# Edge weights of a two-layer graph attention kernel, computed per group of four edge tiles instead of per pair

## The chip, the cores and the metric

The kernel runs on one core of one Trainium2 chip. The metric is device microseconds of that core for one execution; the time given for a kernel is the median of its runs. A core has five engines that run their own instruction queues in order and wait for each other through semaphores: TensorE (PE: matmuls; PEld: its weight loads), VectorE (DVE), ScalarE (ACT), GpSimd (POOL) and SyncE (SP). Data comes from and goes to device memory through DMAs, which SP, ACT and POOL issue.

## The reference

The input is a table x of 6250 nodes with 768 numbers each, and 100000 edges (src, dst), sorted by dst. x is normalised and rectified, goes through two layers of graph attention and two dense layers, and is added to itself. Cut to what matters:

```python
def gat_conv(x, src, dst, W, a_src, a_dst, bias, heads):
    h = (x @ W).reshape(n, heads, -1)
    alpha_s = (h * a_src[None]).sum(-1)
    alpha_d = (h * a_dst[None]).sum(-1)
    e = leaky_relu(alpha_s[src] + alpha_d[dst], 0.2)
    m = segment_max(e, dst);  e = exp(e - m[dst])
    denom = segment_sum(e, dst)
    alpha = e / (denom[dst] + 1e-16)
    return segment_sum(h[src] * alpha[:, :, None], dst).reshape(n, -1) + bias

h = relu(layernorm(x))
h = relu(gat_conv(h, src+loops, dst+loops, W1, ..., heads=4))   # 768 -> 256
h = relu(gat_conv(h, src+loops, dst+loops, W2, ..., heads=1))   # 256 -> 256
out = x + relu(h @ Wm1 + bm1) @ Wm2 + bm2                       # 256 -> 768
```

## The kernel before, in words

**The weight of an edge.** The maximum over a segment cancels in the quotient, so the kernel doesn't subtract it. It also takes a factor out that depends on dst alone: with s the source score and d the destination score, exp(leaky_relu(s + d)) divided by exp(d) is max(exp(s), exp(0.2 s) · rho), with rho = exp(-0.8 d). The weight of an edge is therefore two exponentials of the source score (e1 and e2, on ScalarE), one product with rho and one maximum (both on VectorE). Each source row in the table of a layer carries its score behind its features, so that one gather brings both.

**Stages.** First come the features of all 49 node tiles of 128 nodes (line 414 and after). Then `layer_edges` (line 529) runs once per layer over the edges. Edges are cut into tiles of 128, four tiles make a group, and there are NG = 196 groups, of which the first has only its last two tiles. Groups 4t to 4t+3 share one PSUM tile `e_ps[t]`, in which `meet` puts, through small matmuls with a 0/1 mask, rho of every edge in three bf16 parts, and `join` adds the parts. The later thirds of this tile hold v and, in layer 1, the weight w.

**One group.** The order of work is written out by hand, in the loop from line 706; no scheduler moves it. In iteration g every engine gets its instructions in this order: `gather(g + 8)` issues four indirect DMAs on POOL (line 553), each of which brings 128 rows for one tile of the group eight ahead; `pair(g, 0)` works on the first two tiles of group g; `advance` runs a piece of the work on node tiles that are complete; `make_hot(g + 1)` (layer 1, line 583) builds the 0/1 matrices of the next group; depending on g mod 4 come `meet`, `ahead` (line 785) or, in layer 1, `make_mask` (line 572); then `pair(g, 1)` for the other two tiles, `advance` again, `join` every fourth time, and `gather_up(g - 2)` (lines 673 and 681), which adds the group's sums from PSUM to the running sum.

**A pair.** `pair` issues two exponentials (lines 620 and 622), the product v (line 625) and the maximum w (line 628 in layer 2, line 635 in layer 1). In layer 1 it then scales the two gathered tiles by w in one instruction (line 637), and TensorE multiplies by the 0/1 matrices `hot`. In layer 2 it builds a weighted 0/1 matrix per tile (line 632), and TensorE multiplies it by the gathered rows. Both end in two matmuls per pair into `o_ps` (line 648).

**Buffers.** Gathered rows have 20 buffers of two tiles, ten groups in all. The instructions of a gather wait for the last readers of their buffer, and for the landing of the gather eight before. The small tiles e1, e2 and w have four buffers each, `hw` has eight, `o_ps` three.

**Node work.** When the 128 nodes of a tile are complete, `node.steps` normalises them (lines 791 to 804 in layer 1; 896 to 911 in layer 2), transposes them and multiplies. Layer 1 writes the row table of layer 2 (line 817), from which the gathers of layer 2 read; layer 2 ends in the dense layers and the output (lines 937 to 946). The first few gathers of each layer read only rows that are written early (line 300), and a matmul adds what they miss (lines 273 and 275).

Of the kernel before, what the change touches and what calls it, by code (L numbers as in the profile page):

```python
# [10 lines left out]
F32 = mybir.dt.float32  # L11
BF16 = mybir.dt.bfloat16
I32 = mybir.dt.int32
AF = mybir.ActivationFunctionType
# [3 lines left out]
P = 128  # L18
# [3 lines left out]
HID = 256  # L22
OUT_DIM = 768
SLOPE = 0.2
# [5 lines left out]
TPG = 4  # L30
NG = NQ
# [22 lines left out]
def kernel(  # L54
# [21 lines left out]
    nc = tc.nc  # L76
# [56 lines left out]
    RW = {1: 4 * (HID // 4 + 1), 2: HID + 2}  # L133
# [99 lines left out]
    for layer in EARLY:  # L233
        n = len(THERE[layer])
# [294 lines left out]
    def layer_edges(layer, H, node, pre, matched, pre_pool):  # L529
# [4 lines left out]
        with tc.tile_pool(name=f"eg{layer}", bufs=4) as eg, \  # L534
                tc.tile_pool(name=f"hw{layer}", bufs=8) as hwp, \
                tc.tile_pool(name=f"sum{layer}", bufs=4) as sums, \
                tc.tile_pool(name=f"sm{layer}", bufs=4) as sm:
            G, hot, e_ps, o_ps = {}, {}, {}, {}

            def tiles(g):  # L540

                return range(max(TPG * g, FIRST) - TPG * g, min(TPG * g + TPG, LAST) - TPG * g)
# [61 lines left out]
            def join(t):  # L604
                if t >= NT:
# [4 lines left out]
                    e_ps[t][:, T, 3 * H:4 * H],  # L610
                    e_ps[t][:, T, :3 * H].rearrange("p t (h k) -> p t h k", k=3), AX.X, ALU.add)

            def pair(g, p):

                if 2 * p not in tiles(g):
                    return
                Gp = G.pop(TPG // 2 * g + p)
                sc = Gp[:, :, RW[1]:] if layer == 1 else Gp[:, :, HID:HID + 1]
                e1 = sm.tile([P, 2, H], F32, name="e1")
                nc.scalar.activation(e1, sc, AF.Exp)  # L620
                e2 = sm.tile([P, 2, H], F32, name="e2")
                nc.scalar.activation(e2, sc, AF.Exp, scale=SLOPE)  # L622
                at = TPG * (g % 4) + 2 * p
                rho, v, w = (e_ps[g // 4][:, at:at + 2, k * H:(k + 1) * H] for k in range(3, 6))
                nc.vector.tensor_mul(v, e2, rho)  # L625
                if layer == 2:
                    w = sm.tile([P, 2, H], F32, name="w")
                    nc.vector.tensor_max(w, v, e1)  # L628
                    hw = hwp.tile([P, 2, P], F32, name="hw")
                    for t in range(2):  # L630
                        k = TPG * g + 2 * p + t
                        nc.vector.tensor_scalar(hw[:, t], iota_ps, dcol[:, k:k + 1], w[:, t],  # L632
                                                ALU.is_equal, ALU.mult)
                else:
                    nc.vector.tensor_max(w, v, e1)  # L635
                    hw = hwp.tile([P, 2, H, C + 1], F32, name="hw")
                    nc.vector.tensor_mul(  # L637
                        hw, Gp[:, :, :RW[1]].rearrange("p t (h c) -> p t h c", h=H),
                        w.unsqueeze(3).to_broadcast([P, 2, H, C + 1]))
                if g not in o_ps:  # L640
                    o_ps[g] = ps.tile([P, RW[layer]], F32, name="o_ps", tag="o", bufs=3)
                for t in range(2):
                    k = 2 * p + t
                    if layer == 2:
                        l, r = hw[:, t], Gp[:, t]
                    else:
                        l, r = hot[g][:, k], hw[:, t].rearrange("p h c -> p (h c)")
                    nc.tensor.matmul(o_ps[g], l, r[:, :RW[layer]], start=(k == tiles(g)[0]),  # L648
                                     stop=(k == TPG - 1))
# [56 lines left out]
            for g in range(NG):  # L706
                t, j = divmod(g, 4)
                if g == NG - 2:
                    at_end.append(g)
                gather(g + AHEAD)  # L710
                pair(g, 0)
                if g == NG - 1:
                    pair(g, 1)
# [20 lines left out]
                if g < NG - 1:  # L734
                    pair(g, 1)
# [35 lines left out]
    with tc.tile_pool(name="w2p", bufs=1) as wp, tc.tile_pool(name="wk2", bufs=2) as wk:  # L771
# [48 lines left out]
        with tc.tile_pool(name="pre1", bufs=1) as pre:  # L820
            first_hits(pre, 1, 0)
            pre1 = prepare(pre, 1, 4)
            layer_edges(1, 4, Node1(), pre1,
                        lambda: scores_in(ps, w2, *w2_in, KH, 1), pre)


    with tc.tile_pool(name="wmp", bufs=1) as wp, tc.tile_pool(name="x3", bufs=4) as xp, \
# [122 lines left out]
        for stage in range(2):  # L950
            first_hits(pre, 2, stage)
        layer_edges(2, 1, Node2(), pre2, matched, pre)

    edges_stack.close()
# [298 lines left out]
```

## Time and profile before

| | us |
|---|---|
| median of 3 runs (2609.17 to 2623.1) | 2619.84 |
| profiled execution, its own time | 2137.04 |
| its span, from first to last instruction | 2135.3 |
| POOL busy in the span | 1600.6 |
| PE busy | 1589.5 |
| DVE busy | 1416.1 |
| ACT busy | 593.1 |
| mean granted TensorE clock | 0.825 |

The profile is of one execution. Its own time is 1.7 us above its span, and 482.8 us below the median of the runs: a ratio of 2619.84 to 2137.04, which is 1.226. The page has only one execution in detail, so durations are those of the faster one. "Busy" is the time in which an engine was executing, and not its issuing of instructions. A line of the groups' view names a line of the kernel, the engine and operation, what is written and read with its shape, how often; then the busy time in total and the mean of one in ns, and behind the last bar the idle time of the engine just before these instructions, with what ended it. A line of the timeline gives the start, the duration, the engine, the line and operation, and in brackets the idle time before it.

### The profile page before, as it was taken

The page shows a single profiled execution, that of the slowest core. Times are in us where ns is not written, and L with a number is a line of the kernel's source. Part 1 is how long each engine was busy: PE and PEld are TensorE (multiplying, and loading weights), DVE is VectorE, ACT ScalarE, POOL GpSimd, SP SyncE. Part 2 cuts the span into 40 slices and gives each one's busy share as a digit, 9 for nine tenths or more (in the row PEclk, how much of TensorE's full clock was granted, in tenths as well). Part 3 has the DMA queues.
Part 4 walks back from the last instruction along what each step waited for, and adds up shares of the span by engine and source line. Part 5 has one row for each costly group of instructions (what it writes and reads, how often), then busy time and mean ns, then how long its engine had stood idle before and what let it go on. Part 6 is the DMA issues. An engine that isn't in the chain of part 4 may idle for free.

```text
span 2135.3 us, 26701 instructions
## 1 busy us (share of the span) xinstructions
PE 1589.5 (74%) x6763; PEld 1075.4 (50%) x6765; DVE 1416.1 (66%) x4359; ACT 593.1 (28%) x2601; POOL 1600.6 (75%) x1759
## 2 busy tenths in 40 slices
PE   8996777766767677666768677777767777777777
PEld 6874444444444444444445445545545545545544
DVE  7887777667677777677777655555555555555554
ACT  4651222222222222222222222222222222222222
POOL 6877777777777777777777777777777777777774
PEclk9998888677777767887779888888888888888888
DMA  9976666555555565565556455565555555565553
GB/s 356 363 232 206 169 172 176 165 169 163 167 170 163 170 170 162 169 168 158 166 143 211 130 180 166 169 181 166 169 181 166 169 181 166 169 181 167 168 171 114
DMA packets 157544, 383.26 MB, mean 179 GB/s; under 512 B 35543, under 2 KB 49966, under 8 KB 157382
## 3 DMA queue, kind: packets, MB, share of 16 engines
q0 software_dynamic: 75072, 209.10, 36.6%
q1 hardware_dynamic: 80940, 170.88, 23.1%
q10 hardware_dynamic: 1370, 1.48, 0.2%
q8 instruction: 58, 0.95, 0.2%
q14 instruction: 104, 0.85, 0.1%
HBM read 323.13 MB, written 58.19 MB: 179 GB/s over the span
## 4 chain that ended last, share of the span: by engine, by line
DMA 27%; PE 26%; DVE 26%; issue 9%; ACT 7%; POOL 5%; ACTq 0%; SPq 0%; POOLq 0%; DVEq 0%
DMA G<-table,src_i 26%; PE o_ps L648 11%; DVE hw L637 8%; PE y_ps L937 7%; POOL G L553 4%; PE h_ps L350 4%; DVE acc L673 3%; DVE e_ps L625 3%; ACT sum L681 3%; DVE e_ps L635 2%; ACT e L620 2%; DVE hw L632 2%; DVE mask L572 1%; ACT e L622 1%; PE y_ps L873 1%
## 5 line engine op out<-in xcount | busy, mean ns | idle before, releaser
L553 POOL DMA_INDIRECT G<-table,src_i x1545 | 1470.1, 952 | 472.3 <-issue 260.5
L648 PE MATMUL o_ps<-hw,hot 128*128 128x260 f32 x1564 | 596.7, 520 | 282.9 <-DVE hw L637 221.4
L648 PE MATMUL o_ps<-G,hw 128*128 128x258 f32 x1564 | 469.1, 432 | 229.8 <-DVE hw L632 229.1
L648 PEld LDWEIGHTS o_ps<-hw,hot 128*128 128x128 f32 x1564 | 352.9, 248 | 492.9 <-DVE hw L637 359.2
L625 DVE TENSOR_TENSOR e_ps<-e,e_ps 128x8 f32<-128x8 f32 (+1 forms) x782 | 128.4, 164 | 598.9 <-ACT e L622 597.5
L648 PEld LDWEIGHTS o_ps<-G,hw 128*128 128x128 f32 x1564 | 309.9, 212 | 348.3 <-DVE hw L632 290.5
L681 ACT ACTIVATE sum<-acc 32x260 f32<-32x260 f32 (+1 forms) x384 | 159.9, 416 | 776.9 <-DVE acc L673 775.3
L620 ACT ACTIVATE e<-G 128x8 f32<-128x8 f32 (+1 forms) x782 | 159.9, 204 | 617.8 <-DMA G<-table,src_i 576.4
L632 DVE TENSOR_SCALAR hw<-iota_ps,dcol,w 128x128 f32<-128x128 f32 x782 | 285.0, 406 | 14.4
L637 DVE TENSOR_TENSOR hw<-G,e_ps 128x520 f32<-128x520 f32 x391 | 271.9, 695 | 15.2 <-DVE e_ps L635 2.0
L937 PE MATMUL y_ps<-wm,mT 128*128 128x384 f32 x392 | 206.5, 664 | 0.7 <-ACT mT L926 0.7
L673 DVE SCALAR_TENSOR_TENSOR acc<-acc,keep,o_ps 128x260 f32<-128x260 f32 (+1 forms) x388 | 184.5, 476 | 0.1
L622 ACT ACTIVATE e<-G 128x8 f32<-128x8 f32 (+1 forms) x782 | 148.9, 190 | 0.2
L350 PE MATMUL h_ps<-w,r 128*128 128x256 f32 x588 | 133.0, 380 | 4.4 <-ACT r L341 4.4
L583 DVE TENSOR_TENSOR hot<-iota_ps,dcol 128x512 f32<-128x512 f32 (+1 forms) x196 | 133.5, 682 | 0.0
L937 PEld LDWEIGHTS y_ps<-wm,mT 128*128 128x128 f32 x392 | 88.3, 249 | 66.9 <-issue 40.9
L350 PEld LDWEIGHTS h_ps<-w,r 128*128 128x128 f32 x588 | 108.0, 190 | 21.8 <-ACT r L341 5.7
L635 DVE TENSOR_TENSOR e_ps<-e_ps,e 128x8 f32<-128x8 f32 x391 | 68.1, 174 | 13.4
L365 POOL TENSOR_TENSOR ha<-kept,a1b 128x512 f32<-128x512 f32 x45 | 53.2, 1183 | 23.9 <-ACT kept L356 23.8
L628 DVE TENSOR_TENSOR w<-e_ps,e 128x2 f32<-128x2 f32 x391 | 62.2, 159 | 13.3
L601 PEld LDWEIGHTS <-mask 128*128 128x128 bf16 x1564 | 57.7, 101 | 11.4 <-issue 1.7
L767 ACT ACTIVATE rT<-tp,bT 128x128 f32<-128x128 f32 x196 | 59.4, 352 | 6.6 <-PE tp L761 6.4
(405 smaller groups left out, 1137.7 us busy)
## 6 DMA issues: line engine op xcount, KB each, us to landing
xt<-in_x SPq DMA_DIRECT2D x96, 384.0 KB, 4.8
drow<-dmod_d SPq DMA_DIRECT2D x49, 512.0 KB, 6.4
mask_d<-mask SPq DMA_DIRECT2D x98, 256.0 KB, 2.2
mask<-mask_d SPq DMA_DIRECT2D x98, 256.0 KB, 5.9
G<-table,src_i POOLq DMA_INDIRECT x1545, 2.9
xTt<-in_xT SPq DMA_DIRECT2D x49, 384.0 KB, 5.9
out<-y SPq DMA_DIRECT2D x48, 384.0 KB
table<-kept SPq DMA_DIRECT2D x49, 132.0 KB, 3.7
```

The source lines that it names most:

```text
L350: nc.tensor.matmul(h_ps, r[:, k], w1[:, k], start=(k == 0), stop=(k == KI - 1))
L553: nc.gpsimd.indirect_dma_start(out=G[k // 2][:, k % 2], out_offset=None, in_=table[layer], in_offset=bass.IndirectOffsetOnAxis(ap=src_i[:, ...
L583: nc.vector.tensor_tensor(hot[g][:, T[0]:T[0] + n], iota_ps.unsqueeze(1).to_broadcast([P, n, P]), dcol[:, k:k + n].unsqueeze(2).to_broadca ...
L620: nc.scalar.activation(e1, sc, AF.Exp)
L622: nc.scalar.activation(e2, sc, AF.Exp, scale=SLOPE)
L625: nc.vector.tensor_mul(v, e2, rho)
L632: nc.vector.tensor_scalar(hw[:, t], iota_ps, dcol[:, k:k + 1], w[:, t], ALU.is_equal, ALU.mult)
L637: nc.vector.tensor_mul(hw, Gp[:, :, :RW[1]].rearrange("p t (h c) -> p t h c", h=H), w.unsqueeze(3).to_broadcast([P, 2, H, C + 1]))
L648: nc.tensor.matmul(o_ps[g], l, r[:, :RW[layer]], start=(k == tiles(g)[0]), stop=(k == TPG - 1))
L673: nc.vector.scalar_tensor_tensor(acc, run[0], keep[:, k:k + 1], o_ps.pop(g), ALU.mult, ALU.add)
L681: nc.scalar.activation(done[t][r], acc[r], AF.Copy)
L937: nc.tensor.matmul(y_ps, mT[:, j], wm2[:, j, s * half:(s + 1) * half], start=False, stop=(j == KH - 1))
```

## The change

A new function `weigh(g, pairs)` works out the weights of all tiles of a group at once. It is called from `pair(g, 0)` with both pairs (in group 0 from `pair(0, 1)`, with the only pair that is there), and its results wait in a dictionary for the two pairs. The last two groups (g >= NG - 2) call it once per pair, as before. The exponentials stay one per pair and kind, but all four of a group now stand together, ahead of the first product; the product and the maximum are one instruction each over four tiles. What follows in `pair` is unchanged, and so is the order of the loop around it. The tiles e1, e2 and w are twice as wide, in as many buffers.

```diff
+            def weigh(g, pairs):
+
+                pairs = [p for p in pairs if 2 * p in tiles(g)]
+                n = 2 * len(pairs)
+                e1 = sm.tile([P, TPG, H], F32, name="e1")
+                e2 = sm.tile([P, TPG, H], F32, name="e2")
+                for k, p in enumerate(pairs):
+                    Gp = G[TPG // 2 * g + p]
+                    sc = Gp[:, :, RW[1]:] if layer == 1 else Gp[:, :, HID:HID + 1]
+                    nc.scalar.activation(e1[:, 2 * k:2 * k + 2], sc, AF.Exp)
+                    nc.scalar.activation(e2[:, 2 * k:2 * k + 2], sc, AF.Exp, scale=SLOPE)
+                at = TPG * (g % 4) + 2 * pairs[0]
+                rho, v, w = (e_ps[g // 4][:, at:at + n, k * H:(k + 1) * H] for k in range(3, 6))
+                nc.vector.tensor_mul(v, e2[:, :n], rho)
+                if layer == 2:
+                    w = sm.tile([P, TPG, H], F32, name="w")[:, :n]
+                nc.vector.tensor_max(w, v, e1[:, :n])
+                for k, p in enumerate(pairs):
+                    weights[g, p] = w[:, 2 * k:2 * k + 2]
+
             def pair(g, p):
 
                 if 2 * p not in tiles(g):
                     return
-                Gp = G.pop(TPG // 2 * g + p)
-                sc = Gp[:, :, RW[1]:] if layer == 1 else Gp[:, :, HID:HID + 1]
-                e1 = sm.tile([P, 2, H], F32, name="e1")
-                nc.scalar.activation(e1, sc, AF.Exp)
-                e2 = sm.tile([P, 2, H], F32, name="e2")
-                nc.scalar.activation(e2, sc, AF.Exp, scale=SLOPE)
-                at = TPG * (g % 4) + 2 * p
-                rho, v, w = (e_ps[g // 4][:, at:at + 2, k * H:(k + 1) * H] for k in range(3, 6))
-                nc.vector.tensor_mul(v, e2, rho)
+                if g >= NG - 2:
+                    weigh(g, (p,))
+                elif (g, p) not in weights:
+                    weigh(g, (0, 1))
+                Gp, w = G.pop(TPG // 2 * g + p), weights.pop((g, p))
                 if layer == 2:
-                    w = sm.tile([P, 2, H], F32, name="w")
-                    nc.vector.tensor_max(w, v, e1)
                     hw = hwp.tile([P, 2, P], F32, name="hw")
...
                 else:
-                    nc.vector.tensor_max(w, v, e1)
                     hw = hwp.tile([P, 2, H, C + 1], F32, name="hw")
```

More of the change, by code (lines that the diff above doesn't have):

```diff
@@ L537, in layer_edges @@
                 tc.tile_pool(name=f"sm{layer}", bufs=4) as sm:
-            G, hot, e_ps, o_ps = {}, {}, {}, {}
+            G, hot, e_ps, o_ps, weights = {}, {}, {}, {}, {}
             def tiles(g):
```

## The prediction

> **What bounds the kernel now.** I read the busy shares first, then the waits of POOL, then stretches out of both layers, the groups, and last the timeline. The page has POOL and PE level:
>
> ```profile
> PE 1589.5 (74%) x6763; PEld 1075.4 (50%) x6765; DVE 1416.1 (66%) x4359; ACT 593.1 (28%) x2601; POOL 1600.6 (75%) x1759
> ```
>
> A quarter of POOL seems to be idle. Its waits say what that is (total us, times, longest):
>
> ```profile
> POOL G L553 <- issue: 260.5, 855, 0.4
> POOL G L553 <- ACT e L622: 41.4, 136, 0.3
> POOL G L553 <- PE o_ps L648: 37.5, 123, 0.3
> ```
>
> 855 waits of 0.3 us each, none longer than 0.4, and the others have the same 0.3 us under whatever name happened to be last. That is a fixed cost between two gathers. The timeline of POOL, in both layers, confirms it:
>
> ```profile
> 714.55 0.95 POOL L553 DMA_INDIRECT G<-table,src_i  x1 [0.30 <-issue]
> 715.80 0.95 POOL L553 DMA_INDIRECT G<-table,src_i  x1 [0.30 <-issue]
> ...
> 2109.43 0.95 POOL L553 DMA_INDIRECT G<-table,src_i  x1 [0.30 <-ACT mT L926]
> 2110.68 0.95 POOL L553 DMA_INDIRECT G<-table,src_i  x1 [0.30 <-issue]
> ```
>
> A gather starts every 1.25 us, from 144.6 us to 2110.7 us: 1564 gathers (1545 of line 553, 19 of line 300) x 1.25 = 1955 us, and the stretch is 1966. One real wait is in it, 1.89 us at 1146.8 us between the layers. So the span is 144.6 before the first gather, 1966 of gathers without another pause, and 24.6 after the start of the last. The chain that ended last names POOL's line with 4% only, and the gathers' DMA with 26%, because it follows data; but the data comes when POOL has issued it.
>
> The others have room in each layer (busy us in 200 us of layer 1, then of layer 2, in the order PE, PEld, DVE, ACT, POOL):
>
> ```profile
> 640.00:840.00 200.00, 142.47 (x540) 94.09 (x539) 143.63 (x401) 49.39 (x240) 151.56 (x160) 0.73 0.59 167
> 1440.00:1640.00 200.00, 150.01 (x680) 100.41 (x680) 113.60 (x410) 54.78 (x250) 151.28 (x161) 0.84 0.58 172
> ```
>
> A group takes four gathers, 5.00 us. Of these DVE works 143.63/200 x 5.00 = 3.59 us in layer 1 and 2.84 in layer 2, PE 3.56 and 3.75. They follow the gathers at the heel; nothing holds POOL back.
>
> [...]
>
> ```profile
> 730.57 0.48 DVE L572 TENSOR_SCALAR mask<-drow,pidx 128x1024 bf16<-128x1024 bf16 x1
> 730.80 1.06 POOL L553 DMA_INDIRECT G<-table,src_i  x1 [0.30 <-DVE hot L583]
> ...
> 734.57 0.42 DVE L791 TENSOR_TENSOR all__7316<-mine,sum 128x260 f32<-128x260 f32 x1
> ...
> 734.67 1.14 POOL L553 DMA_INDIRECT G<-table,src_i  x1 [0.30 <-ACT e L622]
> ```
>
> A gather that starts under the mask, or under a sum of two SBUF tiles, comes 1.37 and 1.44 us before its successor. I went through all spacings: 55 are between 1.30 and 2.3 us, and lose 10.3 us together, 0.19 each; nearly all stand beside lines 572, 791, 804, 785 or 896.
>
> **The change, part by part.**
>
> *Removed on DVE.* The groups give
>
> ```profile
> L635 DVE TENSOR_TENSOR e_ps<-e_ps,e 128x8 f32<-128x8 f32 x391 | 68.1, 174 | 13.4
> L625 DVE TENSOR_TENSOR e_ps<-e,e_ps 128x8 f32<-128x8 f32 x391 | 65.0, 166 | 225.7 <-ACT e L622 225.1
> L625 DVE TENSOR_TENSOR e_ps<-e,e_ps 128x2 f32<-128x2 f32 x391 | 63.4, 162 | 373.2 <-ACT e L622 372.4 <-DVE rden L908 0.5
> L628 DVE TENSOR_TENSOR w<-e_ps,e 128x2 f32<-128x2 f32 x391 | 62.2, 159 | 13.3
> ```
>
> Six elements more cost the product 4 ns, 0.67 each; so I estimate 171 and 180 ns at 16 elements, 163 and 160 at 4. A group of layer 1 had 2 x (166 + 174) = 680 ns and will have 351, one of layer 2 642 and 323. With 193 groups that change (not the first and the last two): 193 x (329 + 319) ns = 125 us and 772 instructions fewer. On the path: 0, since POOL's next gather doesn't wait for them. If that cover were gone, they would be worth up to 125 us.
>
> *The exponentials* stay four per group at 190 to 207 ns: 0.
>
> *The added wait.* The product for pair 0 now needs all four gathers, two cadences or 2.5 us more. Behind it in DVE's queue stand the scaling of pair 0, `hot`, the mask, node work and `gather_up`; in ACT's queue, behind the exponentials of pair 1, stand the sums (line 681), rT, o and mT, and PE waits for these. All of it comes up to 2.5 us later, and does again in every group, without adding up: after the landing DVE has 3.59 - 0.33 = 3.26 us of work in 5.00, PE 3.56 or 3.75. Only POOL could turn lateness into time. Its waits are for the readers of a buffer ten groups old (8 groups ahead of use, 40 us) and for the landing of the gather eight before (10 us; landing takes 2.9). 2.5 us don't reach either. Cost 0; without these buffers it would be up to 2.5 x 194 x 2 = 970 us. No DMA is moved on SP's or POOL's queue; stores and masks of SP come up to 2.5 us later, and the masks of layer 2 are read a layer later.
>
> *The seam and the end.* The last two groups of a layer go per pair as before. At the seam the exponentials of layer 1's last pair wait 2.62 us for their data, so a delay of group 193 is used up before it. At the end I count -0.4 to +1 us: the consumer is behind there, and DVE has 0.33 us less to do. Together -1 to +2.5, I take 0.
>
> *Lockout.* [...] 97 masks and four lines of about 49, 293 in all, of which 55 now hit, 19%. Their places against the cadence change. Bounds: none hits, -10 us; all hit, 293 x 0.19 - 10 = +45. In between I argue from the phase. The exponentials that waited for a landing mostly start 0.3 to 0.5 us after a gather's start. All work of a group now starts from there, and a group is exactly four cadences, so that phase is more fixed than before. In an odd group: product at 0.4 + 0.34, scaling of pair 0 at 1.15, `hot` 0.62 later, and the mask at 1.77 + 0.61 = 2.38, which is 1.13 into a cadence, and the next gather starts under it at 1.25. About a quarter of masks hit now; I take half: 97 x 0.25 x 0.19 = +4.6 us. The others I leave, so +4.
>
> Sum, against the profiled execution: 2137 + 0 + 0 + 4 = 2141 us.
>
> **From there to the median.** The median of the runs is 1.226 times the profiled time. [...] I read the runs as the same kernel, bound by the same gathers, at that ratio; no trace here shows it. 2141 x 1.226 = 2624.
>
> **The rivals.** 0.5% is about what a measurement of this kernel can tell from no change: 13 us of the runs, or 10.7 of the profile.
>
> 1. *As forecast*, within 0.5%: 2607 to 2633.
> 2. *Slower through lockout.* The fixed phase puts masks and sums under gathers in most groups. For: above. Against: landings scatter by some us[...]. From 55 hits to 112 it decides: 57 x 0.19 = 10.7 us; all 293 hits would give 2137 + 45 = 2182, or 2675. I put it at about 2645.
> 3. *Faster.* The runs, which no profile shows, are bound by DVE and not by POOL. Then up to 125 x 1.226 = 153 us go: 2467. Against: DVE is at 3.59 of 5.00 us, and would have to be slower by 1.39 times where POOL isn't.
> 4. *Slower through the clock.* PE's work now comes in one burst per group. [...] If it fell below 0.84 x 3.75/5.00 = 0.63 in layer 2, PE would need more than a group's 5.00 us. At 0.5 it needs 6.30: 196 x 1.30 = 255 us, 2137 + 255 = 2392, or 2930. Against: the gap per group is only 5.00 - 3.75 = 1.25 us.
>
> **Chances.** Case 1 has 0.74, case 2 0.17, case 3 0.06 (with lockout gone and more), case 4 0.03. So faster 0.06, same 0.74, slower 0.20. The range of 8 in 10 takes in most of case 2: 2607 to 2650.
>
> **What would show it.** POOL's spacing of 1.25 us and its first and last gather within some us of before, and DVE busy near 1290 us with 3587 instructions, while the span stays: right. What DVE saves should come back as idle time before the product v. More than 112 spacings above 1.30 us, or POOL busy above 1612: case 2. Waits of POOL over 0.4 us, for PE or DVE, in the middle of a layer: the cover that I count on isn't there. PEclk below 0.63: case 4. A median that moves without the profile's span would mean that the runs are bound by something else.

## The result, and the profile after

The changed kernel takes 2647.11 us (median of 4 runs, 2640.82 to 2652.78), beside 2618.53 us for the kernel before (4 runs): a ratio of 1.0117, with an interval of 1.0092 to 1.0142. It is slower by 1.2%. The time lies within the forecast range, but outside the likeliest case, which said no change. The profiled execution of the changed kernel took 2648.64 us, with a span of 2646.9; so this time the profile is one of a run like the timed ones.

The busy shares of the changed kernel:

```profile
PE 1623.4 (61%) x6763; PEld 1120.4 (42%) x6765; DVE 1290.9 (49%) x3587; ACT 561.5 (21%) x2601; POOL 1598.9 (60%) x1759
```

VectorE did 772 instructions and 1416.1 - 1290.9 = 125.2 us less, as forecast. POOL was busy just as long as before, 1598.9 us against 1600.6, yet the span is 511.6 us longer than that of the profile before. POOL stood still instead. The waits (total us, times, longest us) show it, and also where VectorE stood:

```profile
POOL G L553 <- issue: 763.9, 1303, 7.7
...
DVE acc L686 <- remote: 412.9, 48, 17.8
```

In the profile of before POOL's longest wait in this row was 0.4 us; here it is 7.7. The busy time in 200 us of layer 1, then of layer 2 (order PE, PEld, DVE, ACT, POOL):

```profile
640.00:840.00 200.00, 108.60 (x432) 73.30 (x432) 104.56 (x255) 34.64 (x187) 121.01 (x127) 0.72 0.47 132
1440.00:1640.00 200.00, 114.97 (x499) 80.15 (x499) 83.44 (x271) 34.73 (x171) 125.20 (x132) 0.75 0.47 136
```

127 and 132 gathers instead of 160 and 161. No engine is busy throughout. The timeline of POOL and then of VectorE, around one of the pauses of layer 1, shows who waits for whom:

```profile
760.93 0.94 POOL L553 DMA_INDIRECT G<-table,src_i  x1 [0.30 <-issue]
762.17 0.95 POOL L553 DMA_INDIRECT G<-table,src_i  x1 [0.30 <-issue]
769.45 1.07 POOL L553 DMA_INDIRECT G<-table,src_i  x1 [6.33 <-issue]
```

```profile
756.63 0.69 DVE L650 TENSOR_TENSOR hw<-G,e_ps 128x520 f32<-128x520 f32 x1
766.09 0.48 DVE L686 SCALAR_TENSOR_TENSOR acc<-acc,keep,o_ps 128x260 f32<-128x260 f32 x1 [8.77 <-remote]
767.58 0.18 DVE L626 TENSOR_TENSOR e_ps<-e,e_ps 128x16 f32<-128x16 f32 x1 [1.01 <-ACT e L623]
767.79 0.18 DVE L629 TENSOR_TENSOR e_ps<-e_ps,e 128x16 f32<-128x16 f32 x1
768.01 0.70 DVE L650 TENSOR_TENSOR hw<-G,e_ps 128x520 f32<-128x520 f32 x1
```

Where POOL does run, gathers are 0.95 us long and 1.25 us apart, as in the profile before. Then VectorE waits 8.77 us before the sum `acc`, whose input comes from TensorE. POOL goes on until all its buffers are full: counted from the trace, it is then 36 to 40 tiles ahead of the scaling, and 40 is what the buffers hold. At 763.1 us it stops. When `acc` has started at 766.09, the order is `acc`, the sum and four exponentials on ScalarE (from 766.61 to 767.55 us, for which VectorE waits 1.01 us), product, maximum, scaling; only the scaling frees a buffer, and the next gather starts 769.45 - 766.09 = 3.36 us after the start of `acc`. I call this stretch the restart. From this `acc` to the next late one, at 792.36 us, it is 26.3 us, for sixteen gathers that take 20.0. So in these stretches VectorE and what it waits for set the pace, and POOL follows.

"remote" stands where the trace finds no instruction whose end fits the signal that ended the wait. The signal itself is in the trace: it is TensorE's, at 766.06 us, 0.03 us before `acc` starts; five more follow up to 766.36, and none is recorded from 748.48 up to it. TensorE's work had been done long before:

```profile
749.23 1.14 PE L661 MATMUL o_ps<-hw,hot 128*128 128x260 f32 x4 [0.38 <-DVE hw L650]
...
757.68 1.04 PE L661 MATMUL o_ps<-hw,hot 128*128 128x260 f32 x4
768.76 3.56 PE L661 MATMUL o_ps<-hw,hot 128*128 128x260 f32 x8 [10.04 <-DVE hw L650]
```

The matmuls that this `acc` adds up (those of the group two before) end with the first line, at 750.37 us, 15.7 us before `acc` starts, and TensorE is idle from 758.72 us on. VectorE waits over 2 us before `acc` 45 times in layer 1 of this trace, and each time these matmuls had ended 10 to 25 us before. Six signals within 0.3 us can't be the ends of matmuls of which four take 1.1 us. So, by the records of its instructions, TensorE's signals come late here, and not its work.

The profile before shows nothing of this: there POOL led the scaling by some 4 to 8 tiles only, in both layers. It is the profile of a run of another kind than those whose median was given.

### The profile page after: what moved, and what is told of

The parts are those of the page before. It is cut to its first block, busy times and chain, and to the rows that moved or that the text cites. A ratio compares the mean times of both kernels' runs of the same rounds, so it can differ in the third digit from the quotient of the medians.

```text
span 2646.9 us, 25778 instructions
## 1 busy us (share of the span) xinstructions
PE 1623.4 (61%) x6763; PEld 1120.4 (42%) x6765; DVE 1290.9 (49%) x3587; ACT 561.5 (21%) x2601; POOL 1598.9 (60%) x1759
## 4 chain that ended last, share of the span: by engine, by line
issue 24%; DVE 23%; PE 23%; another core or an unknown queue 20%; ACT 7%; DMA 2%; POOL 1%; ACTq 0%; DVEq 0%; SPq 0%; POOLq 0%
PE o_ps L661 10%; DVE hw L650 5%; PE y_ps L950 5%; DVE hot L583 4%; PE h_ps L350 4%; DVE hw L646 3%; ACT sum L694 3%; DVE acc L686 2%; ACT e L622 2%; DVE e_ps L626 2%; DMA G<-table,src_i 2%; PE tp L934 1%; DVE mask L572 1%; ACT e L623 1%
## 5 line engine op out<-in xcount | busy, mean ns | idle before, releaser
L661 PE MATMUL o_ps<-hw,hot 128*128 128x260 f32 x1564 | 573.5, 507 | 562.2 <-DVE hw L650 370.6
L661 PE MATMUL o_ps<-G,hw 128*128 128x258 f32 x1564 | 487.8, 449 | 182.3 <-issue 115.3
L661 PEld LDWEIGHTS o_ps<-G,hw 128*128 128x128 f32 x1564 | 338.3, 226 | 295.7 <-issue 150.9
L686 DVE SCALAR_TENSOR_TENSOR acc<-acc,keep,o_ps 128x260 f32<-128x260 f32 (+1 forms) x388 | 184.7, 476 | 432.4 <-remote 412.9
L626 DVE TENSOR_TENSOR e_ps<-e,e_ps 128x16 f32<-128x16 f32 (+3 forms) x396 | 68.4, 173 | 452.8 <-ACT e L623 228.5
L646 DVE TENSOR_SCALAR hw<-iota_ps,dcol,w 128x128 f32<-128x128 f32 x782 | 274.4, 402 | 7.7 <-issue 0.5
L953 DVE TENSOR_TENSOR y<-y_ps,xt 128x384 f32<-128x384 f32 (+1 forms) x98 | 54.3, 554 | 325.6 <-remote 134.3
L622 ACT ACTIVATE e<-G 128x8 f32<-128x8 f32 (+1 forms) x782 | 153.4, 196 | 72.9 <-issue 40.1
L623 ACT ACTIVATE e<-G 128x8 f32<-128x8 f32 (+1 forms) x782 | 148.5, 190 | 0.0
L934 PE MATMUL tp<-rT,wm 128*128 128x128 f32 x392 | 62.9, 312 | 54.1 <-ACT rT L780 43.1
L934 PEld LDWEIGHTS tp<-rT,wm 128*128 128x128 f32 x392 | 59.2, 222 | 65.0 <-ACT rT L780 49.6
L601 PE MATMUL e_ps<-win,mask 128*128 128x12 bf16 (+1 forms) x1564 | 59.3, 168 | 33.4 <-issue 32.7
## 6 DMA issues: line engine op xcount, KB each, us to landing
mask_d<-mask SPq DMA_DIRECT2D x98, 256.0 KB
mask<-mask_d SPq DMA_DIRECT2D x98, 256.0 KB
```

The source lines that it names most:

```text
L622: nc.scalar.activation(e1[:, 2 * k:2 * k + 2], sc, AF.Exp)
L623: nc.scalar.activation(e2[:, 2 * k:2 * k + 2], sc, AF.Exp, scale=SLOPE)
L686: nc.vector.scalar_tensor_tensor(acc, run[0], keep[:, k:k + 1], o_ps.pop(g), ALU.mult, ALU.add)
L934: nc.tensor.matmul(m_ps[:, j], wm1[:, k, j * P:(j + 1) * P], rT[:, k], start=(k == 0), stop=(k == KH - 1))
```

## The experiments

The runs fell on several chips. On some the kernel before takes about 2575 or 2619 us, and POOL pauses; on others it takes about 2137 us, and POOL never pauses within a layer. I call them pausing and steady chips. No chip whose number is on record showed both kinds, but each was seen for a short time only; whether it is the chip or its state at the time that decides is not shown. A ratio is always to the kernel before on the same chip.

### The kernel before, once more, on a pausing chip

No edit. The kernel before took a median of 2574.66 us on this chip (12 runs).

> The kernel before, unchanged, for a trace of an execution as long as its runs are (2619 us), since the trace of before is of one of 2137. In the changed kernel's trace POOL stands still for 5 to 6 us after every 16 gathers, 510 us together. Wait theory (the change costs because a group's first pair waits for its last gather): this trace has the same pauses, of 480 us together, and the 29 us of difference lie inside them or at the restart after each. Pause theory (the change causes the pauses): few pauses here, and a span near 2140. If it shows pauses, those aren't the change's doing.

One more run took 2578.37 us, with a span of 2576.6. This run pauses too. Its VectorE and POOL, in one of the pauses:

```profile
721.35 0.48 DVE L673 SCALAR_TENSOR_TENSOR acc<-acc,keep,o_ps 128x260 f32<-128x260 f32 x1 [7.23 <-remote]
722.65 0.17 DVE L625 TENSOR_TENSOR e_ps<-e,e_ps 128x8 f32<-128x8 f32 x1 [0.81 <-ACT e L622]
722.86 0.17 DVE L635 TENSOR_TENSOR e_ps<-e_ps,e 128x8 f32<-128x8 f32 x1
723.07 0.70 DVE L637 TENSOR_TENSOR hw<-G,e_ps 128x520 f32<-128x520 f32 x1
```

```profile
717.31 0.95 POOL L553 DMA_INDIRECT G<-table,src_i  x1 [0.30 <-issue]
724.50 1.10 POOL L553 DMA_INDIRECT G<-table,src_i  x1 [6.24 <-issue]
```

The same picture, with a restart of 724.50 - 721.35 = 3.15 us: the product doesn't wait for the two exponentials of pair 1. So the pauses are not the change's doing; the change meets them. All starts of gathers, cut into stretches (us), say where the time lies; a pause is what a spacing has over 1.25 us. The first column is the profile of before, the last one the changed kernel on a steady chip, from an experiment below:

| | before, profiled (steady) | before again (pausing) | after (pausing) | after again (steady) |
|---|---|---|---|---|
| to the first gather | 144.6 | 147.3 | 147.8 | 146.2 |
| 770 gathers of layer 1 | 971.4 | 1179.8 | 1242.2 | 969.5 |
| 30 gathers over the seam | 39.6 | 78.0 | 77.5 | 40.6 |
| the rest, layer 2 | 955.2 | 1122.3 | 1130.8 | 956.2 |
| after the start of the last | 24.6 | 49.1 | 48.6 | 26.0 |
| span | 2135.3 | 2576.6 | 2646.9 | 2138.5 |
| pauses over 3 us in layer 1 | 0 | 30, 157.2 us | 43, 264.1 us | 0 |

The two pausing columns come from different chips, so their difference isn't exact. But most of it lies in layer 1, in longer and more frequent pauses.

### Only the order of the exponentials

The kernel before, in which all four exponentials of a group go ahead of pair 0; products and maxima stay where they were, two of each per group.

```diff
...
+                if (g, p) not in exps:
+                    for q in (p,) if g >= NG - 2 else (0, 1):
+                        if 2 * q in tiles(g):
+                            exponentials(g, q)
...
```

> Only ScalarE's order is moved: all four exponentials of a group stand ahead of its first pair, as in the changed kernel, while product and maximum stay one per pair and in their old places, so that VectorE's first pair doesn't wait for the second pair's rows. Wait theory: the cost is VectorE's wait, so this is near before, within 0.4% (2608 to 2630). Rival, ScalarE's queue: what stands behind the early exponentials (sums, transposed tiles) is what is late, and this is as slow as the changed kernel, 1.0 to 1.3% over before.

2589.93 us, ratio 1.0050 (1.0025 to 1.0076), on the same chip as the run before. So this part of the change alone costs 15 us there, which lies between the two forecasts (up to 0.4%, or 1.0% and more) and decides for neither. The trace has 1195.5 us for the 770 gathers of layer 1, 15.7 more than the kernel before, and 1123.4 for layer 2, 1.1 more. The restart is no longer than before (median 3.15 us), since the product still follows the exponentials of its own pair. Where the 15 us arise is not shown.

### The weights together, but in two instructions each

The changed kernel with its product and maximum cut in two again, all four instructions ahead of the scaling of pair 0.

```diff
-                nc.vector.tensor_mul(v, e2[:, :n], rho)
...
-                nc.vector.tensor_max(w, v, e1[:, :n])
+                for k in range(0, n, 2):
+                    nc.vector.tensor_mul(v[:, k:k + 2], e2[:, k:k + 2], rho[:, k:k + 2])
+                    nc.vector.tensor_max(w[:, k:k + 2], v[:, k:k + 2], e1[:, k:k + 2])
```

> The changed kernel with two products and two maxima per group in place of one of each, all four ahead of the first pair's scaling. So the waits are those of the changed kernel, and nothing of VectorE's 125 us is saved. Wait theory: as slow as the changed kernel or a little slower, 1.0 to 1.8% over before. Rival, the merged instructions (16 elements, or the tile that both pairs share) are what costs: near before, within 0.4%.

2632.11 us, ratio 1.0245 (1.0211 to 1.0278), again on that chip: more than the forecast of 1.0 to 1.8%, and far from the rival's 0.4%. VectorE and POOL in one of its pauses:

```profile
629.54 0.48 DVE L687 SCALAR_TENSOR_TENSOR acc<-acc,keep,o_ps 128x260 f32<-128x260 f32 x1 [7.55 <-remote]
...
631.73 0.69 DVE L651 TENSOR_TENSOR hw<-G,e_ps 128x520 f32<-128x520 f32 x1
```

```profile
625.86 0.95 POOL L553 DMA_INDIRECT G<-table,src_i  x1 [0.30 <-issue]
633.17 1.07 POOL L553 DMA_INDIRECT G<-table,src_i  x1 [6.37 <-issue]
```

The restart is 633.17 - 629.54 = 3.63 us. The 770 gathers of layer 1 took 1230.2 us, 50.4 more than the kernel before; layer 2 took 1121.8, 0.5 less. So on a pausing chip it costs time to put pair 1's product and maximum ahead of pair 0's scaling: 42 us more than the exponentials alone, with no instruction added to the kernel. The merged form has the same place and two instructions fewer, and its ratio, on another chip, is 1.0117. I read the difference as what merging gives back, about 1.3%; on one and the same pausing chip this wasn't measured.

The restart doesn't explain the size. Its median over the late `acc` of layer 1 is 3.15 us in the kernel before (22 of them), 3.15 with the exponentials first (31), 3.36 in the changed kernel (42) and 3.63 here (39). 49 pauses, one for every four groups of layer 1, with 0.48 us more would be 24 us, where 50.4 were measured, and the exponentials cost 15.7 with no longer restart. What grows is the waiting for late signals of TensorE. In the order before, exponentials first, this kernel:

```profile
DVE acc L673 <- remote: 185.3, 33, 11.7
...
DVE acc L685 <- remote: 203.4, 37, 11.7
...
DVE acc L687 <- remote: 317.2, 45, 14.0
```

In the changed kernel it is 412.9 us in 48 waits. In layer 1 alone, all waits of VectorE over 2 us sum to 255.6 us in the kernel before and 303.4 here, 47.8 more; the rest of VectorE's time, from the first scaling to the last, is 920.4 and 924.9. In the changed kernel, on another chip, the two are 388.8 and 846.9: outside its long waits VectorE is 73 us faster, as it should be with 193 x 0.33 = 64 us less work, but the waits are 133 us longer. Why this order meets more late signals, or later ones, is not settled.

### TensorE's small matmuls spread

I suspected that a burst of TensorE's work makes `acc` late: the sixteen small matmuls of `meet`, which stand together once in four groups. This is the kernel before with four of them per group.

```diff
-                    meet(t + 1)
...
+                meet(t + 1, (j,))
```

> The kernel before with the 16 small matmuls of one node tile spread over the four groups before they are needed, four to each, in place of all in one burst. In the changed kernel's trace the pauses come at the rate of these bursts, one per four groups. If the bursts cause the pauses: these shrink by more than half, and the time falls below 2400 us. If they don't: 2600 to 2640 us, with the pauses still every 16 gathers.

2644.72 us, ratio 1.0280 (1.0246 to 1.0315). The pauses did not go; 42 over 3 us with 256.0 us in layer 1. VectorE now waited ahead of `join` rather than of `acc`, with the same "remote" (405.8 us in 54 waits). The burst isn't their cause. Why this kernel is 2.8% slower than the one before, no run says.

### The changed kernel, on two steady chips

No edit to the changed kernel.

> The changed kernel itself, beside the next three. Theory R (restart): in the runs all gather buffers are full, and about once per four groups POOL stands still until VectorE's sum acc is released; then only the time from that release to the next gather counts, 98 times in both layers. The change puts two more exponentials of 0.1 us into that stretch, 98 x 0.21 = 20 us: ratio to before 1.008 to 1.014, the time from the end of acc to the next gather about 3.4 us. Theory C (chain): VectorE's and ScalarE's chain is the bound in every one of the 392 groups; then the change should move -0.33 + 0.2 us per group, about -50 us: 0.98. The prediction's theory (gathers are the bound, the order of the consumers is covered): 1.000.

> The changed kernel once more. The chip decides: where the kernel before takes about 2137 us and gathers run without a pause, 1.000 to 1.002 of it. Where the kernel before takes 2570 to 2620 us and POOL's gathers pause, theory R (98 restarts, two more exponentials of 0.1 us in each): 1.008 to 1.014, and about 3.4 us from the end of acc to the next gather; theory W (VectorE waits for rows of later gathers): the same ratio.

2139.58 us, ratio 1.0013 (1.0003 to 1.0022), and 2139.25 us, ratio 1.0009 (1.0001 to 1.0018), beside 2137.58 and 2136.88 us for the kernel before. On these chips the change costs 2 us. The first run's profile took 2140.23 us. It has the picture on which the prediction was built. The page, the head of POOL's waits, POOL's timeline and the windows in both layers:

```profile
PE 1531.8 (72%) x6764; PEld 1061.4 (50%) x6765; DVE 1277.6 (60%) x3587; ACT 578.8 (27%) x2601; POOL 1600.1 (75%) x1759
```

```profile
POOL G L553 <- issue: 253.1, 831, 0.3
```

```profile
714.24 0.94 POOL L553 DMA_INDIRECT G<-table,src_i  x1 [0.30 <-issue]
715.49 0.95 POOL L553 DMA_INDIRECT G<-table,src_i  x1 [0.30 <-ACT e L623]
```

```profile
640.00:840.00 200.00, 131.82 (x541) 88.85 (x541) 130.08 (x320) 45.82 (x240) 151.52 (x160) 0.78 0.60 167
1440.00:1640.00 200.00, 150.05 (x682) 101.33 (x681) 99.43 (x332) 54.65 (x250) 151.27 (x161) 0.88 0.57 172
```

160 and 161 gathers in 200 us, as before; VectorE has 13.6 and 14.2 us less in the same time. The groups show where that went:

```profile
L629 DVE TENSOR_TENSOR e_ps<-e_ps,e 128x16 f32<-128x16 f32 x193 | 35.2, 182 | 6.7
L626 DVE TENSOR_TENSOR e_ps<-e,e_ps 128x16 f32<-128x16 f32 x193 | 34.6, 179 | 304.8 <-ACT e L623 304.6
L626 DVE TENSOR_TENSOR e_ps<-e,e_ps 128x4 f32<-128x4 f32 x193 | 32.3, 167 | 457.5 <-ACT e L623 455.4 <-ACT e L622 2.1
L629 DVE TENSOR_TENSOR w<-e_ps,e 128x4 f32<-128x4 f32 x193 | 31.2, 162 | 6.6
```

The idle time before the product was 225.7 + 373.2 = 598.9 us and is 304.8 + 457.5 = 762.3. VectorE waits longer for the same gathers.

### The weights one group earlier

If the restart is what counts, it can be cut: the changed kernel, with the weights of group g + 1 worked out at the end of iteration g, ahead of `acc`. The scaling can then follow `acc` at once.

```diff
+                if g + 1 < NG - 2:
+                    weigh(g + 1, (0, 1))
                 if g < NG - 2:
                     gather_up(g - 2)
```

> The changed kernel with the weights of group g+1 worked out at the end of iteration g, ahead of the sum acc; the same instructions, only their place moves. After acc is released the scaling of pair 0 can start at once. Theory R: the restart falls from about 3.4 us to about 2 us, 98 x 1.4 = 137 us less than the changed kernel: ratio to before 0.95 to 0.97. Theory C: 1.4 us less in each of 392 groups until the gathers at 1.25 us are the bound: below 0.90. Theory W (what costs is that VectorE waits for rows of later gathers): it waits for still later rows, so no faster than the changed kernel, 1.01 to 1.03.

> The changed kernel with the weights of group g+1 worked out at the end of iteration g, ahead of acc; the same instructions, only their place moves. On a chip where gathers run without a pause: 1.000 to 1.002 of before. On one where they pause, theory R: the restart falls from about 3.4 us to about 2 us, and with 98 restarts up to 137 us go: 0.95 to 0.97 of before. Theory C (VectorE's and ScalarE's chain bounds each of 392 groups): below 0.90. Theory W: it waits for still later rows, no faster than the changed kernel, 1.01 to 1.03.

> The same kernel as in the run before (weights of group g+1 at the end of iteration g, ahead of acc), in the hope of a chip on which POOL's gathers pause. Where the kernel before takes about 2137 us: 1.000 to 1.002. Where it takes 2570 to 2620 us, theory R (98 restarts of 3.4 us, of which this takes 1.4): 0.95 to 0.97; theory C (every one of 392 groups is bound by the consumers' chain): below 0.90; theory W (waiting for rows of later gathers costs): 1.01 to 1.03.

All three fell on steady chips: ratios 1.0009 (1.0002 to 1.0015), 1.0010 (1.0003 to 1.0018) and 1.0000 (0.9991 to 1.0009). They say that this order costs nothing there, and say nothing of the pausing chips, for which the kernel was made. Whether it beats the kernel before on one of those is open.

### hot built in VectorE's gap

The changed kernel, with `make_hot(g + 1)` ahead of `pair(g, 0)` in layer 1.

```diff
                 gather(g + AHEAD)
+                if g <= NG - 4:
+                    make_hot(g + 1)
                 pair(g, 0)
...
-                if g <= NG - 4:
-                    make_hot(g + 1)
```

> The changed kernel with the 0/1 matrices of the next group (hot, 0.68 us of VectorE, layer 1 only) built before pair 0 instead of after it, in the 1.0 us in which VectorE waits for the exponentials. Theory R: in a restart VectorE is idle there anyway, and the way to the next gather is as long as before; so the time of the changed kernel within 10 us, 1.00 to 1.02 of before. Theory C: 0.62 us less in each of 193 groups, 120 us: 0.96 to 0.97 of before.

2139.44 us, ratio 1.0008 (0.9999 to 1.0017), on a steady chip, where both theories have nothing to say. Inconclusive for them.

### Fewer buffers

The kernel before with 12 buffers of two gathered tiles for 20.

```diff
-AHEAD = 8
+AHEAD = 4
```

> The kernel before with AHEAD = 4 for 8: 12 buffers of gathered rows instead of 20, so gathers run at most six groups ahead instead of ten. Theory R: POOL stands still at every restart however many buffers there are, since it fills them all between two: within 0.5% of before, gathers ahead of the scaling by about 20 to 24 tiles instead of 36 to 40. The prediction's theory (the depth of buffers covers lateness of the consumers): with 40% fewer buffers more lateness reaches POOL, slower by over 1%.

2142.02 us, ratio 1.0023 (1.0014 to 1.0031), on a steady chip. Layer 1 took 976.3 us for 971.4. Most of that is one wait of 4.06 us before the 25th gather, at 181.4 us: the first 24 tiles had filled the twelve buffers. After that POOL led by a few tiles, as in the kernel before, so the two theories about full buffers aren't tested. What follows is smaller: with the consumers at the heel, the sixteen tiles of buffers that this run lacks count at the start of the layer only.

### How deep the cover is

The changed kernel with two more instructions like `hot` in layer 1, once per group between the maximum and the scaling; their result isn't used.

```diff
+                if layer == 1 and n == TPG:
+                    for _ in range(2):
+                        nc.vector.tensor_tensor(
+                            eg.tile([P, TPG, P], F32, name="spare", bufs=1),
+                            iota_ps.unsqueeze(1).to_broadcast([P, TPG, P]),
+                            dcol[:, :TPG].unsqueeze(2).to_broadcast([P, TPG, P]), ALU.is_equal)
```

> The changed kernel with two more instructions like hot (0.68 us each, 1.3 us together; their result is not used) in layer 1, once per group between the maximum w and the scaling of pair 0. It asks how deep the cover is on a chip where gathers run without a pause. Theory B (the prediction's measure: VectorE's busy time, 3.26 us of 5.00 per group, so that 4.6 us still fit): within 5 us of before, no pauses of POOL. Theory K (the consumers' chain counts with its idle time: v to v takes 4.2 to 4.4 us when they are behind, of which 1.0 us is VectorE waiting for acc, sum and exponentials one after the other): 5.5 to 5.7 us per group, over 5.00, so 193 x 0.5 to 0.7 = 100 to 135 us more, ratio 1.047 to 1.063, with the gather buffers full and POOL pausing in layer 1 alone. Where the chip is one on which gathers pause anyway: theory R (98 restarts, 49 of them in layer 1) 49 x 1.3 = 64 us over the changed kernel, 1.03 to 1.04 of before; theory C (every group bound by the chain) 193 x 1.3 = 250 us, 1.10 or more.

2249.01 us, ratio 1.0527 (1.0510 to 1.0545), on a steady chip: 112 us more, as the theory that counts the chain with its idle time said (100 to 135), and not within 5 us, as VectorE's busy time said. VectorE over one group, and the windows of both layers:

```profile
701.87 0.18 DVE L626 TENSOR_TENSOR e_ps<-e,e_ps 128x16 f32<-128x16 f32 x1 [0.88 <-ACT e L623]
702.09 0.18 DVE L629 TENSOR_TENSOR e_ps<-e_ps,e 128x16 f32<-128x16 f32 x1
702.18 1.41 DVE L632 TENSOR_TENSOR spare<-iota_ps,dcol 128x512 f32<-128x512 f32 x2
...
705.70 0.48 DVE L692 SCALAR_TENSOR_TENSOR acc<-acc,keep,o_ps 128x260 f32<-128x260 f32 x1
707.19 0.18 DVE L626 TENSOR_TENSOR e_ps<-e,e_ps 128x16 f32<-128x16 f32 x1 [1.01 <-ACT e L623]
```

```profile
640.00:840.00 200.00, 133.81 (x491) 90.31 (x490) 160.64 (x364) 41.16 (x223) 141.52 (x147) 0.72 0.54 153
1440.00:1640.00 200.00, 147.59 (x685) 100.10 (x685) 98.69 (x329) 54.30 (x250) 151.28 (x160) 0.89 0.57 172
```

This group takes 707.19 - 701.87 = 5.32 us, and with the next three it is 21.99 us, 5.50 a group (5.5 to 5.7 were forecast), over the 5.00 of four gathers, although VectorE is busy for only 160.64 of 200 us. The missing 0.9 to 1.0 us per group is the wait for `acc`, ScalarE's sum and the exponentials, which follow one another in this order of work. POOL's lead in layer 1 is mostly 33 to 40 tiles: the buffers are full. 62.0 us of the loss lie in the 770 gathers of layer 1 (1033.4 against 971.4), and 46.8 at the seam (86.4 against 39.6), where the backlog of the consumers has to be worked off before layer 2. In layer 2, which has no extra work, POOL is steady again (147 gathers in the first window, 160 in the second). And the longest wait of POOL's gathers within layer 1 is 2.0 us: full buffers alone don't bring the waits of 7 us that a pausing chip has.

## Why the prediction was right and wrong

**What bounds the kernel: right for the profile that was read, wrong for the runs that were timed.** On steady chips gathers are 1.25 us apart with no pause, before and after the change, and my sum of 2141 us stands against 2139.58 and 2139.25 (and 2140.23 for the profiled execution).

**Removed on DVE: right.** 125 us and 772 instructions were forecast and measured. The four instructions came out at 179, 182, 167 and 162 ns, where I had estimated 171, 180, 163 and 160. What was saved came back as idle time before the product, 163 us.

**The added wait: 0 on a steady chip, as forecast,** inside the 2 us of the whole change. Its cover was measured wrongly, though. I set VectorE's busy time of 3.26 us against 5.00. The last experiment shows that the chain with its 1.0 us of idle time counts. When the consumers are behind, it takes 4.1, 4.1, 4.4 and 4.6 us from product to product in the four groups of a cycle (the profile after on a steady chip, early in layer 1), 4.3 on average. So the slack is about 0.7 us per group in layer 1, not 1.7. That the change fitted in because it shortens VectorE's part and merely waits for rows is my reading, and not tested by itself.

**The seam and the end: right** on steady chips, 40.6 and 26.0 us against 39.6 and 24.6.

**Lockout, +4 us: wrong, it is 0.** What the prediction calls lockout is, in the traces, that some gathers which start under a mask or a sum are longer (1.06 and 1.14 us for 0.95 in the profile of before); that VectorE holds POOL up there was my reading, and is not shown. Spacings that lose up to 0.5 us sum to 9.8 us before and 9.7 and 10.0 us after on steady chips. Rival 2, which needed 57 more of them, is out: POOL's busy time is 1600.1. I can't place the 2 us that the change does cost there.

**"From there to the median": this is the step that failed.** I carried the profile over to the median with one factor, 1.226, as if each gather took that much longer in the timed runs; that was an estimate from the two times alone, and no trace showed it. The measurement decides against it. At 2647 us a gather takes 950 ns and `hot` 682 ns, as at 2140 us (951 and 682). POOL and VectorE run no slower; POOL stands still, since its buffers are full. In those runs the gathers don't bound the kernel, and the cover on which every zero of mine rested isn't there. The prediction said that waits of POOL over 0.4 us in the middle of a layer would show just that, and they do: 7.7 us. That 2647 lies in the range all the same is luck: the range went beyond 2633 for the sake of the lockout, which measured 0.

**Rival 3 had the premise and missed the sign.** It said that the runs are bound by something other than POOL, and gave VectorE's 125 us as the gain. But VectorE isn't full there either, at 49%. In layer 1 the change does shorten VectorE's time outside its long waits, by 73 us; the waits for late signals of TensorE grow by 133 us (both across two chips), and the restart goes from 3.15 to 3.36 us. Two parts of the change are shown on one pausing chip: the exponentials together cost 0.5%, and pair 1's weights ahead of pair 0's scaling some 2% more. That merging gives 1.3% back, so that 1.2% is left, is worked out across two chips. Rival 4 is out: the granted clock in 200 us of layer 2 of the changed kernel is 0.75 on the pausing chip and 0.88 on a steady one, not below the 0.63 that I had estimated. That bursts of TensorE's work lower the clock was my assumption, and is not shown.

**What stays open** is why TensorE's signals come late on a pausing chip, and why the changed order waits longer for them. Bursts of `meet` aren't it, and full buffers alone aren't. In the changed kernel's trace from the pausing chip 547 of 1442 recorded signals of TensorE come more than 1.5 us after the end of its last instruction that sends one; on the steady chip it is 2 of 1672. One thing goes along with it: the traces of pausing chips hold 13,230 to 14,119 records of semaphore signals, those of steady ones some 42,000 to 43,000. Whether the fewer records and the late signals have one cause, no run here shows.

## What to carry to other kernels

Before a forecast is scaled from a profile to a median that is 23% away, ask whether it is the same kernel in both: if gathers would take 1.25 us in both, the rest is standing still, and its cause has to be found. When a trace gives a wait no releaser, look at when the work that it waits for had ended; here it was 15.7 us before. When work is grouped, count what moves ahead of the first instruction that frees a buffer, not only what is saved; working out the weights of pair 1 ahead of the scaling of pair 0 cost 2.5% unmerged and, on another chip, 1.2% merged where the buffers are full, and 0.1% where they are not. Measure slack by the time from one group to the next, idle time within included, and not by busy time.

## What the runs showed of the hardware that was not expected

The same program takes 2137 us on some chips and 2575 to 2619 on others, at equal durations of its gathers and of `hot`. The difference is made of waits, up to 17.8 us before `acc` in the changed kernel. They are for signals of TensorE: in layer 1 each `acc` that waited over 2 us starts 10 to 25 us after the end of its matmuls. Full buffers only put a delay off: in the last experiment POOL ran some 33 tiles further ahead than in the kernel before, and the gathers over the seam between the layers took 46.8 us longer (86.4 against 39.6), about the 41 us that 33 gathers take at 1.25 us.
